# Eight or seven row tiles of a sparse neighbour sum by mask matmuls, the rest by indirect transfers

## The chip, the cores and the metric

One Trainium2 chip, one core of it. A core has five engines that run their own instruction streams: PE (TensorE, matmuls), DVE (VectorE), ACT (ScalarE), POOL (GpSimd) and SP (SyncE), and 16 DMA engines that they feed. The metric is the device time of one execution in microseconds (us), and smaller is better. Times inside an execution are counted from the start of the span, which reaches from the first to the last instruction of the program.

## The reference

Two graph layers over N = 4096 nodes with D = 512 features, float32. The adjacency `adj` is symmetric with the diagonal set and with a chance of about 0.002 for any other pair, so a row has some 9 neighbours on average and 24 at most in the lists below.

```python
h = relu(layernorm(x))
# layer 0: 8 heads; of a row's neighbours the one with the highest score gives its values
attn = softmax(Q K^T * scale + energy, over the neighbours)
x = x + (attn == max(attn)) / 8 @ V
# layer 1: mean over the neighbours, two linear maps, a third over both
h = relu(layernorm(x))
agg = mask @ h / deg
x = x + relu(concat(h @ W_self + b_self, agg @ W_nb + b_nb) @ W_comb + b_comb)
```

The last line is where this document plays: with the weights folded, layer 1 needs `G = h @ wN` for every node and then, for every row, the sum of G over the row's neighbours, times 1/degree, plus the row's own part.

## The kernel before, in words

`sparse_path` does the whole work; `general_path` stands behind a flag for denser inputs and isn't run here. The nodes are sorted by degree, falling. The order is in `perm`, and the sorted rows are cut into 32 tiles of 128 rows. `CAPS[r]` (L509) is the length of the neighbour lists of tile r, with the row itself in slot 0: 24 for tile 0, 11 for tiles 7 to 9, 5 for tile 31.

The kernel has three parts. The first (to about 340 us) reads adj, computes keys and values, packs the adjacency into words and makes the lists. The words are the point here: `W_d` holds for each row 256 words, and bit s of word j (with an offset) says whether node 256 s + j is a neighbour; s runs over NPL = 16 planes. The second part (to about 1075 us) is layer 0 and the products of layer 1, tile by tile; its last steps write G to `G_d` in HBM and the rows' own parts to `X1_d`, fetch the words of the first DENSE tiles (`dense_words`, L1417) and turn them (`dense_turn`, L1424) into `wT`, word by row.

The third part (L1629 to L1740) makes the neighbour sums in two ways at once.

- **By mask**, for tiles 0 to DENSE-1. For each plane s: `dense_mask(s)` (L1638, DVE) shifts one bit of all words to where it reads as the float 2.0 and drops the rest; `dense_keys(s)` (L1648, a DMA on ACT's queue) loads the 256 rows of G of this plane; `dense_sum(s)` (L1655, PE) multiplies, two matmuls per tile and plane, and adds up in one PSUM bank per tile. Masks and keys have three buffers each, so mask s waits until PE has ended plane s-3.
- **By transfers**, for tiles DENSE to 31. For each of the CAPS[r]-1 list places POOL issues one indirect DMA (L1719, in the helper `gather`, L1103) that fetches 128 rows of G. The rows land in `room`, which has three places, taken by r % 3. DVE adds them up (`total`, L1682; for the last tile `halved`, L1691), and `finish` (L1672, L1673) multiplies, adds the own part and the residual. `put` (L1119) scatters the finished tile to the output with another indirect DMA on POOL.

Everything in this part is issued in the order in which the loop at L1713 writes it. After tile r's transfers POOL issues the put of tile r-2; then come tile r's sum and finish on DVE; then, as long as `calls >= pace * (s - 2)`, one more mask and its matmuls, where `calls` counts list transfers plus one for each tile done. Three masks are issued ahead of the loop. So a mask stands on DVE's queue between the finish of one tile and the sum of the next, and a put on POOL's queue holds back all transfers behind it until DVE has finished that tile. In the last pass, POOL's last transfers are followed by the finishes and puts of the first half of the mask tiles, then by tile 31, then by the other half (L1723 to L1739).

Of the kernel before, what the change touches and what calls it, by code (L numbers as in the profile page):

```python
# [512 lines left out]
LISTV = CAPS[VTILE]  # L513
FIRST = 4
GMAX = 10
DENSE = 8
MAGIC = 0x5F3759DF


# [18 lines left out]
def sparse_path(  # L538
# [91 lines left out]
    with ExitStack() as pa:  # L630
# [299 lines left out]
        def on(step, t, *args):  # L930
            if 0 <= t < KT:
                step(t, *args)
# [159 lines left out]
    with ExitStack() as pb:  # L1092
# [9 lines left out]
        def gather(dst, src, idx, at=0):  # L1102
            last[0] = nc.gpsimd.indirect_dma_start(  # L1103
                out=dst, out_offset=None, in_=src,
                in_offset=bass.IndirectOffsetOnAxis(ap=idx, axis=0), element_offset=at,
            )
            if at:

                beyond.append(last[0])
                for w in written:  # L1110
                    tc.declare_no_dep(last[0].ins, w.ins, reason="other columns")
# [305 lines left out]
        def dense_words():  # L1417

            wg = gp.tile([P, DENSE, SEG], F32, tag="kg", name="wg")
            for r in range(DENSE):  # L1420
                gather(wg[:, r, :], W_d[:, :], perm[:, r : r + 1])
            return wg

        def dense_turn(wg):  # L1424

            wT = wp.tile([P, 2, DENSE, P], I32, tag="w_a", name="wT")
            for a in range(0, DENSE, 2):
                pt = pst.tile([P, NC, P], F32, tag="tr", name="tr")
                for h in range(2):
                    for b in range(2):  # L1430
                        nc.tensor.transpose(pt[:, 2 * h + b, :], wg[:, a + b, ts(h, P)], ident)
                nc.vector.tensor_copy(
                    wT[:, :, a : a + 2, :], pt.rearrange("p (h b) q -> p h b q", h=2)
                )
            return wT

# [4 lines left out]
        left, last_tiles, m = apart[FIRST:], fused[-3:], KT - FIRST - 3  # L1441
# [22 lines left out]
        for r in turns:  # L1464
            p = pos[r]
# [28 lines left out]
        def late(step, kind, i, *args):  # L1494

            out_ = []
            for r in turns:
                if plan[kind].get(r) == i:
                    out_ += step(r, *args) or []
            return out_  # L1500
# [22 lines left out]
        for i in range(-5, KT):  # L1523
# [9 lines left out]
            a, b = on(key_gathers, i), late(value_gathers, "value", i)  # L1533
# [86 lines left out]
        fi = cp.tile([1, 1], I32, tag="fi", name="fi")  # L1620
        nc.vector.tensor_copy(fi, fps)
        wT = dense_turn(wg)
        for r in tail:
            s = st[r]
# [4 lines left out]
    with ExitStack() as pd:  # L1629
# [4 lines left out]
        order.enter_context(tc.manual_schedule())  # L1634
        dacc = [psd.tile([P, D], F32, tag=f"da{r}", name="da") for r in range(DENSE)]
        masks, keys = {}, {}

        def dense_mask(s):  # L1638

            mk = gp.tile([P, 2, DENSE, P], F32, tag="mk", name="mk")  # L1640
            nc.vector.tensor_scalar(
# [66 lines left out]
        s = ahead  # L1708
        calls = 0

        pace = 11
        x1s = {}
        for r in range(DENSE, KT):  # L1713
            n = CAPS[r] - 1
# [29 lines left out]
def kernel(tc, *args):  # L1744
    left = sparse_path(tc, *args)
    with tc.If(left > 0):
        general_path(tc, *args)
# [40 lines left out]
```

## Time and profile before

| | us |
|---|---|
| median of 6 runs (lowest to highest) | 1421.24 (1417.43 to 1425.43) |
| the profiled execution's own time | 1419.52 |
| its span | 1417.8 |
| first transfer of the third part, POOL | 1077.46 |
| first and last matmul of the masks, PE | 1114.19 and 1373.1 |
| end of the last list transfer on POOL | 1388.5 |
| mean granted TensorE clock | 0.853 of full speed |

How to read the profile. A page gives, for each engine, its busy time; a picture of the span in 40 slices; the chain of work that ended last; and groups of instructions, one line each: code line, engine, operation, what it writes from what it reads, how many, then busy us and the mean ns of one, then the idle time of the engine ahead of them and what ended it. A view of waits adds up who waited for whom: us in total, times, the longest. A timeline gives single instructions in order: start, duration, engine and line, and in brackets the idle time ahead and its releaser. A table by windows gives, for each stretch of time, each engine's busy time with the number of its instructions, the granted clock, and the share of time in which the DMA engines were busy. A releaser called "issue" means that the engine waited for nothing that the profile shows; "remote" means that the semaphore's change could not be matched to an instruction that ended just then. A float32 matmul leaves two records, so 512 records are 256 matmuls, and a plane of eight tiles is 32 records.

### The profile page before, as it was taken

The page shows a single profiled execution, that of the slowest core. Times are in us where ns is not written, and L with a number is a line of the kernel's source. Part 1 is how long each engine was busy: PE and PEld are TensorE (multiplying, and loading weights), DVE is VectorE, ACT ScalarE, POOL GpSimd, SP SyncE. Part 2 cuts the span into 40 slices and gives each one's busy share as a digit, 9 for nine tenths or more (in the row PEclk, how much of TensorE's full clock was granted, in tenths as well). Part 3 has the DMA queues.
Part 4 walks back from the last instruction along what each step waited for, and adds up shares of the span by engine and source line. Part 5 has one row for each costly group of instructions (what it writes and reads, how often), then busy time and mean ns, then how long its engine had stood idle before and what let it go on. Part 6 is the DMA issues. An engine that isn't in the chain of part 4 may idle for free. (4 is left out here: it accounts for less than half of the span.)

```text
span 1417.8 us, 10765 instructions
## 1 busy us (share of the span) xinstructions
PE 1071.9 (76%) x2918; PEld 487.7 (34%) x2918; DVE 991.3 (70%) x1650; ACT 427.8 (30%) x880; POOL 776.2 (55%) x910
## 2 busy tenths in 40 slices
PE   5998989867763658567788767777889597989870
PEld 3554545423321223222333222333333242434330
DVE  5568786883594498878787787777572494859495
ACT  5787766612200333232333323332531000000000
POOL 2322313244677476666766666667445654775574
PEclk9999999989985778778887778888899797998895
DMA  9999998295765377777777777767555986786763
GB/s 363 419 421 420 419 360 306 99 363 209 221 190 152 95 245 212 227 234 236 229 228 226 218 223 223 224 209 219 208 178 155 354 306 200 237 260 204 233 220 130
DMA packets 109222, 350.09 MB, mean 247 GB/s; under 512 B 18064, under 2 KB 18064, under 8 KB 100960
## 3 DMA queue, kind: packets, MB, share of 16 engines
q0 software_dynamic: 63376, 208.23, 47.3%
q1 hardware_dynamic: 39552, 129.78, 23.7%
q10 hardware_dynamic: 6224, 11.31, 2.4%
q8 instruction: 25, 0.41, 0.1%
q14 instruction: 45, 0.37, 0.1%
HBM read 285.25 MB, written 68.19 MB: 249 GB/s over the span
## 5 line engine op out<-in xcount | busy, mean ns | idle before, releaser
L1660 PE MATMUL da<-gk,mk 128*128 128x512 f32 x512 | 237.8, 622 | 36.8 <-issue 21.3
L628 PE MATMUL q<-wq,hqT 128*128 128x512 f32 x256 | 156.8, 718 | 142.2 <-issue 123.6
L1103 POOL DMA_INDIRECT kg<-K_d,sidx x177 | 170.2, 961 | 76.3 <-issue 54.1
L1103 POOL DMA_INDIRECT room<-G_d,sidx x174 | 176.7, 1015 | 58.0 <-issue 55.7
L1227 DVE TENSOR_REDUCE sc<-pr 128x32 f32<-128x2048 f32 (+3 forms) x114 | 183.3, 1608 | 3.9
L1660 PEld LDWEIGHTS da<-gk,mk 128*128 128x128 f32 x512 | 101.6, 199 | 173.0 <-issue 173.0
L1682 DVE TENSOR_REDUCE acc<-room 128x512 f32<-128x4096 f32 (+5 forms) x23 | 152.5, 6628 | 4.5 <-DMA room<-G_d,sidx 4.4
L1103 POOL DMA_INDIRECT o<-K_d,vi x128 | 123.3, 963 | 39.1 <-issue 38.7
L628 PE MATMUL pg<-swN,hT 128*128 128x512 f32 x216 | 124.1, 728 | 19.6 <-ACT hT L1347 17.4
L628 PEld LDWEIGHTS q<-wq,hqT 128*128 128x128 f32 x256 | 53.3, 218 | 216.3 <-issue 197.1
L628 PE MATMUL pk<-wk,room 128*128 128x512 f32 x256 | 121.1, 617 | 4.4 <-ACT room L810 4.2
L1103 POOL DMA_INDIRECT room<-K_d,sidx x102 | 99.5, 976 | 32.8 <-issue 26.8
L628 PE MATMUL pv<-wv,room 128*128 128x512 f32 x256 | 115.2, 601 | 0.0
L1224 DVE TENSOR_TENSOR pr<-q,kg 128x2048 f32<-128x2048 f32 (+3 forms) x51 | 102.4, 2007 | 1.4
L1360 PE MATMUL pr<-swS,hT 128*128 128x512 f32 x216 | 99.9, 605 | 0.0
L1224 DVE TENSOR_TENSOR pr<-q,room 128x2048 f32<-128x2048 f32 (+3 forms) x42 | 66.8, 1590 | 42.3 <-issue 24.9
L1119 POOL DMA_INDIRECT G_d<-gs,perm x32 | 31.7, 989 | 104.2 <-ACT gs L1366 69.4
L1224 DVE TENSOR_TENSOR pr<-q,km 128x512 f32<-128x512 f32 x21 | 14.4, 687 | 102.5 <-remote 96.6
L1366 ACT COPY gs<-pg 128x512 f32<-128x512 f32 x27 | 15.7, 582 | 226.6 <-remote 214.3
L628 PEld LDWEIGHTS pg<-swN,hT 128*128 128x128 f32 x216 | 49.3, 237 | 99.2 <-issue 65.2
L1260 DVE COPY_PREDICATED o<-best,room 128x512 f32<-128x512 int32 x102 | 74.3, 728 | 5.9 <-DVE o L1260 1.9
L749 ACT ACTIVATE mkt<-adjt,sgb 128x2048 bf16<-128x2048 int32 x37 | 74.2, 2005 | 12.8 <-POOL adjt L670 12.6
(222 smaller groups left out, 1542.6 us busy)
## 6 DMA issues: line engine op xcount, KB each, us to landing
adjt<-adj_dram SPq DMA_DIRECT2D x37, 1024.0 KB
room<-adj_dram SPq DMA_DIRECT2D x27, 1024.0 KB
x<-X_d SPq DMA_DIRECT2D x32, 512.0 KB
xt<-x_dram SPq DMA_DIRECT2D x32, 256.0 KB
K_d<-ks POOLq DMA_DIRECT2D x32, 256.0 KB
X_d<-xo SPq DMA_DIRECT2D x32, 256.0 KB
X_d<-own SPq DMA_DIRECT2D x32, 256.0 KB
gk<-G_d ACTq DMA_DIRECT2D x16, 512.0 KB
```

Of the source, the lines that this page charges most:

```text
L628: nc.tensor.matmul(dst, h[:, c, :], w[:, c, :], start=(c == 0), stop=(c == NC - 1))
L749: nc.scalar.activation(mk, st[t]["adj"][j], AF.Sigmoid, bias=sgb, scale=400.0, accum_out=degs[:, t, j : j + 1],)
L1103: last[0] = nc.gpsimd.indirect_dma_start(out=dst, out_offset=None, in_=src, in_offset=bass.IndirectOffsetOnAxis(ap=idx, axis=0), element_o ...
L1119: new = nc.gpsimd.indirect_dma_start(out=dst, out_offset=bass.IndirectOffsetOnAxis(ap=perm[:, r : r + 1], axis=0), in_=src, in_offset=None,)
L1224: nc.vector.tensor_tensor(pr[:, :g, :], s["q"].unsqueeze(1).to_broadcast([P, g, D]), kk, ALU.mult)
L1227: nc.vector.tensor_reduce(sc[:, g0 : g0 + g, :], pr[:, :g, :].rearrange("p g (h d) -> p g h d", h=H), AX.X, ALU.add,)
L1260: nc.vector.copy_predicated(s["o"].rearrange("p (h d) -> p h d", h=H), best[:, k, :].bitcast(I32).unsqueeze(2).to_broadcast([P, H, HD]), b ...
L1360: nc.tensor.matmul(pr, s["hT1"][:, c, :], wS[:, c, :], start=False, stop=(c == NC - 1))
L1366: nc.scalar.copy(s["gs"], s["pg"])
L1660: nc.tensor.matmul(dacc[r], masks[s][:, h, r, :], keys[s][:, h, :], start=(s == 0 and h == 0), stop=(s == NPL - 1 and h == 1),)
L1682: nc.vector.tensor_reduce(acc, g[:, 0:n, :].rearrange("p n f -> p f n"), AX.X, ALU.add)
```

## The change

DENSE goes from 8 to 7. Tile 7, with 10 list places, joins the tiles that are summed by transfers: the loop starts at 7, and 184 list transfers are issued in place of 174. The masks, their matmuls, the words fetched and turned, the accumulators and the last finishes are of seven tiles. `dense_turn` works in pairs of tiles and so learns to treat a last single one. And `pace` goes from 11 to 13: a new plane of masks is issued for every 13 counted calls. Of the 16 planes, 13 are issued in the loop; before, those were due after tiles 8, 9, 11, 12, 13, 14, 15, 16, 18, 19, 20, 22 and 23, and now they are due after tiles 8, 9, 10, 11, 13, 14, 15, 17, 18, 20, 22, 23 and 25.

```diff
-DENSE = 8
+DENSE = 7
...
             for a in range(0, DENSE, 2):
                 pt = pst.tile([P, NC, P], F32, tag="tr", name="tr")
+                m = min(2, DENSE - a)
                 for h in range(2):
-                    for b in range(2):
+                    for b in range(m):
                         nc.tensor.transpose(pt[:, 2 * h + b, :], wg[:, a + b, ts(h, P)], ident)
                 nc.vector.tensor_copy(
-                    wT[:, :, a : a + 2, :], pt.rearrange("p (h b) q -> p h b q", h=2)
+                    wT[:, :, a : a + m, :],
+                    pt.rearrange("p (h b) q -> p h b q", h=2)[:, :, 0:m, :],
                 )
...
-        pace = 11
+        pace = 13
```

## The prediction

> **What bounds the kernel now.** I read the chain of work that ended last first, because it says which engines carry the end:
>
> ```profile
> issue 3%; POOL 2%; DVE 2%; DMA 1%; POOLq 0%; DVEq 0%
> POOL room L1103 2%; DVE acc L1682 1%; DVE x L1672 1%; DMA room<-G_d,sidx 1%; DMA out_dram<-x,perm 0%; POOL out_dram L1119 0%; DVE x L1673 0%; DVE room L1691 0%; POOLq L1741 0%; DVEq L1682 0%; POOLq L1119 0%; DVEq L1691 0%; DVEq L1672 0%
> ```
>
> It runs along POOL's transfers and DVE's sums; no matmul is on it. Then the page's groups, for the price of one instruction:
>
> ```profile
> L1660 PE MATMUL da<-gk,mk 128*128 128x512 f32 x512 | 237.8, 622 | 36.8 <-issue 21.3
> ...
> L1103 POOL DMA_INDIRECT room<-G_d,sidx x174 | 176.7, 1015 | 58.0 <-issue 55.7 <-DMA room<-G_d,sidx 1.3 <-DMA out_dram<-x,perm 1.0
> ...
> L1682 DVE TENSOR_REDUCE acc<-room 128x512 f32<-128x4096 f32 (+5 forms) x23 | 152.5, 6628 | 4.5 <-DMA room<-G_d,sidx 4.4
> ```
>
> A list transfer costs POOL (176.7 + 58.0) / 174 = 1.35 us with the issue time ahead of it. Then the waits from 1077 us to the end:
>
> ```profile
> DVE mk L1641 <- remote: 56.9, 3, 20.8
> ...
> POOL out_dram L1119 <- DVE x L1673: 54.0, 11, 15.8
> DVE mk L1641 <- PE da L1660: 21.7, 4, 13.5
> ```
>
> The reader should see two waits that belong together: masks on DVE wait for PE, and POOL's puts wait for DVE. DVE's timeline and POOL's, around the longest pair:
>
> ```profile
> 1174.96 0.69 DVE L1673 SCALAR_TENSOR_TENSOR x<-x 128x512 f32<-128x512 f32 x1
> 1196.46 1.23 DVE L1641 TENSOR_SCALAR mk<-wT 128x2048 int32<-128x2048 int32 x1 [20.81 <-remote]
> 1197.60 8.01 DVE L1682 TENSOR_REDUCE acc<-room 128x512 f32<-128x4608 f32 x1
> ```
>
> ```profile
> 1190.67 0.95 POOL L1103 DMA_INDIRECT room<-G_d,sidx  x1 [0.30 <-issue]
> 1207.40 1.72 POOL L1119 DMA_INDIRECT out_dram<-x,perm  x1 [15.78 <-DVE x L1673]
> ```
>
> Mask 6 stands on DVE from 1175.65 to 1196.46; behind it wait tile 13's sum and finish, behind that its put, and behind that POOL's whole queue. POOL stops so four times: 10.53, 15.78, 11.91 and 12.45 us, 50.7 in all. So **POOL carries the third part, and PE, through the masks, decides when POOL stops**. The windows show how PE looks in three of the stops:
>
> ```profile
> 1143.00:1178.00 35.00, 35.00 (x83) 15.51 (x82) 30.83 (x11) 0.00 (x0) 26.81 (x27) 1.00 0.82 272
> 1178.00:1197.00 19.00, 9.45 (x15) 3.22 (x14) 0.54 (x1) 0.00 (x0) 10.53 (x11) 0.67 0.63 203
> ...
> 1264.00:1281.00 17.00, 9.84 (x15) 3.23 (x14) 2.12 (x2) 0.00 (x0) 9.43 (x10) 0.67 0.73 221
> ...
> 1330.00:1342.00 12.00, 7.04 (x11) 2.21 (x10) 0.87 (x1) 0.00 (x0) 5.50 (x6) 0.69 0.61 200
> ```
>
> The first number after the stretch's length is PE's busy time with its records. At full pace a record comes each 0.429 us (35.0 us hold 83); in these stretches 15, 15 and 11 come where 44, 40 and 28 would. Why PE crawls there no row says. But each crawl ends just after POOL has run dry: POOL's last transfers end at 1191.62, 1276.17 and 1337.03, and the waiting masks start at 1196.46, 1278.88 and 1341.13, that is 4.8, 2.7 and 4.1 us later. In the second part it is the same (POOL's last transfer ends at 625.9, ACT's wait for PE at 630.62). I take it that PE is held until POOL's transfers have drained. From POOL's restart to the first plane whose end is told late, by the counted records, are 16 to 29, 35 to 49 and 21 to 35 us. The first stop (10.53) is of another kind: PE started at 1114.19, mask 3 asked for plane 0 at 1117.4 and got it at 1130.88.
>
> **The change part by part.** All against the span of 1417.8 us.
>
> *Transfers.* Ten more, 10 x 1.35 = 13.5 us on POOL, which carries the path; one put more ahead of the last transfer, 1.3 (0.99 and 0.30 of issue). Sum +14.8. Without the stretched ones, 10 x 1.25 + 1.3 = 13.8 is the low end.
>
> *The first stop goes.* Mask 3 was due after the first looped tile, now after the second. By then DVE has done two sums (8.74 and 8.94 us) and two finishes, about 1127.5; plane 0 of 28 records ends near 1114.2 + 6 x 0.855 + 22 x 0.429 = 1128.8. The put that needs tile 8 comes at about 1131. So -10.5; at worst 9 us of it stay, if PE starts later.
>
> *Matmuls and pace.* A plane has 28 records, 12.0 us in place of 13.7; a plane is due per 13 calls, 13 x 1.35 = 17.6 us in place of 14.9. PE, which runs about three planes behind at first, gains: without stalls plane k ends near 1128.8 + 12.0 k, so planes 6, 9 and 12 near 1201, 1237 and 1273. Masks 9, 12 and 15, which ask for them, come after tiles 15, 20 and 25, at 1077.5 + 82, 120 or 153 transfers at 1.35 + 7, 12 or 17 puts at 1.3 + some 4 of landing + sum and finish (8.7, 7.8, 6.9): near 1210, 1267 and 1317. The lead grows from 9 over 30 to 44 us (less where a plane itself waits for its mask). So the short waits (2.1, 2.1 and 3.9 us in before) go, which carried no stop, and a stall shows later on DVE. It still shows, if PE is released only when POOL stops. In before POOL's runs from restart to stop were 49, 69 and 49 us. I take 35 to 48 us to a stall, as in the longest one, and 20 us of running on, as after 1172: with both running from 1114 a first stop near 1175, a restart near 1190, a second stop with the lead of then near 1280, a restart near 1295. POOL then has 1280 - 1077 - 15 = 188 of its 275 us behind it, and some 75 ahead; the last mask is issued 50 ahead of its end, 25 us after the restart, sooner than a third stall. So **two of the three stall stops stay and one goes**: -13.4, their mean. The ends: none goes (0), or all go (-40.1), the latter if a stall has its own length and isn't ended by POOL.
>
> *Masks on DVE.* Each is an eighth shorter (1.23 to about 1.08 us). The trace shows POOL transfers stretched wherever a mask runs beside them (2.33, 1.82, 1.45, 1.59, 1.55 against a median of 0.95), about 8.7 us over all; an eighth is -1.1. [...]
>
> *The tail.* From the last transfer's end to the span's end are 29.3 us, of which the dense finishes go at 1.39 each, one after the other: one fewer, -1.4. Three of seven now stand ahead of tile 31, four behind.
>
> *At nothing:* one fetch of words fewer (1.26 on POOL at the end of the second part) lies ahead of POOL's wait of 10.8 us for ACT; without that cover it would be -1.3. Two transposes and half a copy fewer in `dense_turn` run on PE and DVE while POOL already transfers; uncovered, under 1 us. DVE's extra sum (8.8) and ACT's and SP's queues, unchanged in number, lie beside POOL: per tile of 9 places DVE needs 8.05 + 1.5 and POOL 12.6. A PE that waits for masks late in the part will start them cold. The row: after 15.1 us of idling the first six records came 0.855 us apart, 2.6 us lost. [...] The sum takes nothing for it, as POOL has longer than PE there.
>
> Sum: 1417.8 + 14.8 - 10.5 - 13.4 - 1.1 - 1.4 = 1406.2. The profiled execution's own time is 1.7 over its span, and the median of the runs 1.7 over that: 1409.6, told as 1410.
>
> **Rivals.** (1) *Three stops stay.* For it: restart to stall took 16 to 29 us once, and PE is as busy as before until about 1270. Then 13.4 comes back: 1423, which is no change. (2) *One stall stop or none.* For it: the late lead of 30 to 44 us is longer than the longest mask wait, 20.8. Against it: the crawls ended with POOL's run and not after a fixed time. One stop: 1396; none: 1383. (3) *PE ends last, slower.* The place is the end: the last mask leaves after tile 25, with 31 transfers and 6 puts left, 31 x 1.35 + 6 x 1.3 = 49.7 us. PE may then have three planes, 36 + 2.6 us, 11 us less than POOL. If a crawl begins once no mask waits, nothing stops POOL and PE stays held until the last transfer lands; of 84 records some 20 were still done after a stall began, and 64 x 0.429 = 27.5 us of matmuls remain ahead of the finishes of the mask tiles. That adds up to 28: 1438 with two stops. It decides from a crawl that takes more than those 11 us. Against it: in before PE ended at 1373.1 and 15 us ahead of POOL. (4) *The change doesn't do what it says*: the instruction order shows 224 matmuls for 256, 184 transfers for 174 and 7 word fetches for 8, so no.
>
> **How the numbers follow.** Two stops 0.42 (1410), three 0.25 (1423), one or none 0.16 (1396, 1383), PE last or a fourth stop 0.17 (1438 and about that). A measurement of this kernel tells 0.3% from no change, 4.3 us. Faster (under 1417): one or none, and most of two stops, 0.53. Within: most of three stops and the upper edge of two, 0.20. Slower: the rest of three, and PE last, 0.27. The range reaches from one stop to PE last, 1394 to 1438; the two-stop case alone, with its unknown sizes, spans 1403 to 1418.
>
> **What would show it.** Right: 448 mask records; no POOL stop near 1132; 184 transfers at about 1.35; two waits of puts over 10 us; POOL's last transfer near 1378 and PE's last matmul ahead of it. Wrong: three or four such waits; a wait of a finish for PE after the last transfer (rival 3); "remote" mask waits with no stop of POOL, or stops with no late PE, which would break the coupling I assume.

## The result, and the profile after

The changed kernel takes 1433.75 us (median of 17 runs, 1424.77 to 1463.17), against 1422.29 us for the kernel before in the 38 runs made beside it. The ratio is **1.0077, 95% interval 1.0054 to 1.0101**: 0.8% slower, some 11 us. The forecast was 1410 us and faster. The medians of the runs of before lie between 1422 and 1432 us in the groups below, so all comparisons go by the ratio to the runs of before on the same chip. Some executions of a kernel take a few per cent longer than the rest (up to 1480.54 us for the kernel before), and the ratios leave them out.

The profiled execution of the changed kernel has a span of 1440.4 us, which is long among its runs: 22.6 us over that of before, where the typical difference is 11. The chain of work that ended last, again by engine and by line:

```profile
DVE 3%; issue 2%; another core or an unknown queue 1%; POOL 1%; DMA 1%; POOLq 0%; DVEq 0%
DVE acc L1684 2%; POOL room L1103 1%; DVE x L1674 1%; DMA out_dram<-x,perm 1%; DMA room<-G_d,sidx 0%; DVE x L1675 0%; DVE room L1693 0%; DVE mk L1643 0%; POOLq L1743 0%; DVEq L1684 0%; POOLq L1119 0%; POOL out_dram L1119 0%; DVEq L1674 0%; DVEq L1693 0%
```

Still no matmul in it, but an entry that before did not have: 1% for "an unknown queue". It is one piece of 20.15 us, from 1343.33 to the start of a mask at 1363.51: the wait of that mask for PE. The groups:

```profile
L1662 PE MATMUL da<-gk,mk 128*128 128x512 f32 x448 | 220.9, 644 | 77.9 <-issue 51.0
...
L1103 POOL DMA_INDIRECT room<-G_d,sidx x184 | 183.2, 995 | 57.8 <-issue 54.2
```

The counts are those announced: 448 records, 184 transfers. PE is busy 17 us less, but idles 77.9 us ahead of its records instead of 36.8: it has less to do and is later with it. The waits from 1077 us to the end (in all, times, longest):

```profile
DVE mk L1643 <- remote: 69.9, 3, 26.3
...
POOL out_dram L1119 <- DVE x L1675: 47.0, 11, 15.9
PE da L1662 <- DMA gk<-G_d: 26.9, 1, 26.9
DVE own L1372 <- remote: 22.7, 1, 22.7
...
POOL out_dram L1119 <- DMA x<-X_d: 20.0, 1, 20.0
```

Three long mask waits are still there, each longer (20 to 26 us, before 18 to 21). And the first stop did not go; it is 20.0 us. It has another cause than before, and it lies ahead of all masks. DVE's timeline shows it:

```profile
1097.81 0.75 DVE L1372 SCALAR_TENSOR_TENSOR own<-gs,smeta,pr 128x512 f32<-128x512 f32 x1 [3.99 <-issue]
1121.22 0.75 DVE L1372 SCALAR_TENSOR_TENSOR own<-gs,smeta,pr 128x512 f32<-128x512 f32 x1 [22.67 <-remote]
1124.22 3.10 DVE L1643 TENSOR_SCALAR mk<-wT 128x1792 int32<-128x1792 int32 x3 [2.25 <-DMA X_d<-own]
...
1136.89 0.69 DVE L1675 SCALAR_TENSOR_TENSOR x<-x 128x512 f32<-128x512 f32 x1
```

And POOL's timeline shows the puts that end the first two stops:

```profile
1137.86 1.01 POOL L1119 DMA_INDIRECT out_dram<-x,perm  x1 [19.99 <-DMA x<-X_d]
...
1204.02 1.59 POOL L1119 DMA_INDIRECT out_dram<-x,perm  x1 [14.43 <-DVE x L1675]
```

The "own" products are the rows' own parts, the last work of the second part: PE multiplies, and DVE takes the product up when PE's semaphore tells it that the product is done (the notice). They come every 4.7 us until the last, the fifth, which DVE gets at 1121.22 although PE's last record of it starts at 1101.80. Behind it stand masks 0 to 2, tile 7's sum, its finish (ended at 1137.58) and, on POOL, its put at 1137.86. The profile puts that 19.99 us to the load of x; the timeline says that the put followed the finish at once. POOL's last transfer had ended at 1117.87, 3.3 us before DVE got the product: the same pair as in the three mask stops.

In those too it is the notice that is late, and not the plane. Here are the start of PE's timeline, in which a run of matmuls without a gap is one line, and two of the three waiting masks:

```profile
1129.27 48.61 PE L1662 MATMUL da<-gk,mk 128*128 128x512 f32 x108 [26.87 <-DMA gk<-G_d]
1179.14 0.59 PE L1662 MATMUL da<-gk,mk 128*128 128x512 f32 x1 [1.26 <-issue]
```

```profile
1193.21 1.09 DVE L1643 TENSOR_SCALAR mk<-wT 128x1792 int32<-128x1792 int32 x1 [23.40 <-remote]
...
1290.41 1.09 DVE L1643 TENSOR_SCALAR mk<-wT 128x1792 int32<-128x1792 int32 x1 [26.28 <-remote]
```

They are masks 5 and 10, which wait for planes 2 and 7. A plane is 28 records, so plane 2 is the first 84 records, done near 1167; mask 5 asks for it at 1169.8 and starts at 1193.21. Seven slow records follow the first 108, and then 114 without a gap up to 1245.5, so plane 7 (record 224) was done near 1243, 47 us ahead of mask 10. Plane 11, by the same count, was done near 1329, 34 us ahead of mask 14 at 1363.51. The matmuls themselves slow down only after these planes, from 1178, 1246 and 1340 on. So a spell has two signs, first notices that don't come, then records far apart. "PE is held" below means such a spell.

Broken down for POOL, from its first list transfer to its last (gaps of its timeline over 2.6 us count as stops):

| | before | after |
|---|---|---|
| first list transfer starts, us | 1077.46 | 1080.35 |
| first stop | 10.5 | 20.0 |
| other stops | 15.8, 11.9, 12.4 | 14.4, 15.9, 13.0 |
| the rest (transfers, puts, small gaps) | 260.4 | 267.9 |
| from the last transfer's end to the end | 29.3 | 28.8 |

So 12.7 of the 22.6 us of this profile are longer stops (9.5 of them the first), 7.5 are the transfers and the put, 2.9 the later start, and 0.5 came back in the tail.

### The profile page after: what moved, and what is told of

It is laid out like the page before. It is cut to its first block, busy times and chain, and to the rows that moved or that the text cites. A ratio compares the mean times of both kernels' runs of the same rounds, so it can differ in the third digit from the quotient of the medians.

```text
span 1440.4 us, 10657 instructions
## 1 busy us (share of the span) xinstructions
PE 1043.2 (72%) x2852; PEld 474.1 (33%) x2852; DVE 997.2 (69%) x1651; ACT 427.7 (30%) x880; POOL 782.1 (54%) x918
## 5 line engine op out<-in xcount | busy, mean ns | idle before, releaser
L1662 PE MATMUL da<-gk,mk 128*128 128x512 f32 x448 | 220.9, 644 | 77.9 <-issue 51.0
L628 PE MATMUL q<-wq,hqT 128*128 128x512 f32 x256 | 147.9, 691 | 123.7 <-issue 101.7
L1103 POOL DMA_INDIRECT room<-G_d,sidx x184 | 183.2, 995 | 57.8 <-issue 54.2
L1684 DVE TENSOR_REDUCE acc<-room 128x512 f32<-128x4096 f32 (+5 forms) x24 | 161.2, 6717 | 8.1 <-DMA out_dram<-x,perm 3.1
L1662 PEld LDWEIGHTS da<-gk,mk 128*128 128x128 f32 x448 | 91.3, 204 | 207.5 <-issue 207.2
L1103 POOL DMA_INDIRECT room<-K_d,sidx x102 | 100.1, 981 | 33.6 <-issue 26.5
L749 ACT ACTIVATE mkt<-adjt,sgb 128x2048 bf16<-128x2048 int32 x37 | 74.2, 2007 | 12.6 <-POOL adjt L670 12.4
L1224 DVE TENSOR_TENSOR pr<-q,km 128x512 f32<-128x512 f32 x21 | 14.4, 685 | 88.9 <-remote 47.0
```

Of the source, the lines that this page charges most:

```text
L628: nc.tensor.matmul(dst, h[:, c, :], w[:, c, :], start=(c == 0), stop=(c == NC - 1))
L749: nc.scalar.activation(mk, st[t]["adj"][j], AF.Sigmoid, bias=sgb, scale=400.0, accum_out=degs[:, t, j : j + 1],)
L1103: last[0] = nc.gpsimd.indirect_dma_start(out=dst, out_offset=None, in_=src, in_offset=bass.IndirectOffsetOnAxis(ap=idx, axis=0), element_o ...
L1224: nc.vector.tensor_tensor(pr[:, :g, :], s["q"].unsqueeze(1).to_broadcast([P, g, D]), kk, ALU.mult)
L1662: nc.tensor.matmul(dacc[r], masks[s][:, h, r, :], keys[s][:, h, :], start=(s == 0 and h == 0), stop=(s == NPL - 1 and h == 1),)
L1684: nc.vector.tensor_reduce(acc, g[:, 0:n, :].rearrange("p n f -> p f n"), AX.X, ALU.add)
```

## The experiments

Kernels e1 to e3 and e5 were run together on one chip, then e4 and e6 to e8 on another, then e9 to e12, then e13 and e14.

### Which half of the change costs: e1 and e2

```
e1 = before, with          e2 = after, with
-        pace = 11         -        pace = 13
+        pace = 13         +        pace = 11
```

> Eight mask tiles, a plane per thirteen transfers (only the pace of the change). Theory T (the loss is the ten transfers and one put, 14.8 us on POOL; POOL's stops add up to the same as in the kernel before, some 50 us, whatever the pace): no change against the kernel before, 1418 to 1427 us, and again four stops of POOL over 10 us. Rival P (the slower pace makes the stops longer, as in the profile of the changed kernel, where they add up to 63 us against 50.7): 1428 to 1438 us. What the prediction held (pace 13 takes the first stop and one more away): 1395 to 1408 us.

Measured: 1413.24 us, ratio 0.9958 (0.991 to 1.0006). Rival P falls. The pace alone does not cost; by the value it **gains 6 us**, though the interval just reaches no change. Theory T's four stops are not there either. The waits:

```profile
DVE mk L1641 <- remote: 47.2, 3, 22.4
POOL out_dram L1119 <- DVE x L1673: 35.4, 11, 15.2
```

Two stops are left, 15.2 and 13.8 us. POOL's first run goes on past 1132 with a pause of 1.9 us only. So with eight tiles the pace did to the stops what the prediction said of it: the first goes, and one of the three others.

> Seven mask tiles, a plane per eleven transfers (only the tile of the change). Theory T: the loss is all here, 1430 to 1438 us, with four stops of POOL over 10 us. Rival P: 1418 to 1428 us, since PE has an eighth less to do per plane at the old pace and the transfers are paid back by shorter stops.

Measured: 1431.8 us, ratio 1.0132 (1.009 to 1.0175). Theory T holds by the time: the loss is all in the seven tiles, some 19 us. But its sum is too small (14.8 less 2.5), and the stops are not those of before: three over 10 us in place of four (18.5, 16.5 and 14.5, and one of 4.8), and for the first of them DVE waits 20.3 us for the last own product, as in the changed kernel. By the values, the pace (0.42% less) and the tile (1.32% more) nearly add up to the whole change (0.77% more).

### Is PE held until POOL stops: e3, e5 and e4

```
e3:  mk = gp.tile(..., tag="mk", name="mk")   ->   ..., name="mk", bufs=6)
```

> The changed kernel with six buffers for mask planes instead of three: mask s waits for plane s-6 in place of s-3. Theory H (PE is held while POOL's transfers run and is let go only when they stop): PE gets slow 35 to 40 us after POOL's restart and stays slow until a mask wait stops POOL, one or two planes later than now; stops get fewer (two), PE ends later: 1415 to 1440 us. Theory L (a slow spell of PE has its own length of 15 to 50 us, whatever POOL does): three planes of slack, 3 x 17.6 = 53 us, cover all of them: no stop of POOL over 5 us but the first, 1385 to 1400 us.

Measured: 1435.24 us, ratio 1.0152 (1.0112 to 1.0191). Theory L falls: three planes more of slack make it slower.

```profile
POOL out_dram L1119 <- DVE x L1675: 63.6, 11, 17.9
...
DVE mk L1643 <- PE da L1662: 30.4, 1, 30.4
...
DVE mk L1643 <- remote: 22.3, 1, 22.3
```

POOL's run after the first stop lasts 111 us in place of 52, and PE is slow for the last 67 of them; then it stops 17.5 us, and 13.9 later. Two stops, as theory H has it, and what is saved in stops is lost at the end: PE's last record starts at 1431.7, 23 us after POOL's last list transfer.

```
e5:  mask s >= 3 is written to a tile of its own that nobody reads;
-    dacc[r], masks[s][:, h, r, :], keys[s][:, h, :]
+    dacc[r], masks[s % 3][:, h, r, :], keys[s][:, h, :]
```

> The changed kernel, but PE multiplies masks 0, 1 and 2 over and over, and DVE writes the later masks, at the same places and cost, into tiles that nobody reads; so DVE and POOL never wait for PE before the end. Leaves out: the right masks of planes 3 to 15. Theory H (PE is let go only by a stop of POOL): POOL runs through to about 1375, PE is slow (a record in 2.1 us) from some 40 us after its start to POOL's end, and has some 260 of 448 records, 110 us, left then: 1470 to 1510 us. Theory L (slow spells of their own length): PE needs 193 us and some spells of 20 us each, ends near POOL: 1380 to 1405 us, no stop of POOL but the first.

Measured: 1503.52 us, ratio 1.0644 (1.0595 to 1.0693); **theory H, inside its range**. PE in four stretches (length, PE busy with its records, PEld, DVE, ACT, POOL, then the granted clock, the DMA share and GB/s):

```profile
1130.00:1160.00 30.00, 30.00 (x71) 13.30 (x70) 29.79 (x13) 0.00 (x0) 23.03 (x23) 1.00 0.91 329
1200.00:1230.00 30.00, 10.11 (x10) 3.14 (x11) 21.54 (x9) 0.00 (x0) 22.99 (x24) 0.50 0.74 231
1300.00:1330.00 30.00, 10.11 (x10) 3.16 (x11) 22.28 (x12) 0.00 (x0) 23.30 (x23) 0.50 0.68 212
1400.00:1430.00 30.00, 30.00 (x71) 13.26 (x70) 0.00 (x0) 0.00 (x0) 0.00 (x0) 1.00 0.17 52
```

PE starts at full pace, drops to a record in 3 us some 45 us after POOL's restart, and stays there for 200 us, with nothing that it waits for, until POOL is done (1360.4). Records follow each other without a gap again from 1372. POOL ran 233 us without a stop, and the finishes of the mask tiles then waited 114 us for PE.

A rival is near at hand: the granted clock is halved in these stretches. But at the half clock records came 0.855 us apart in the kernel before (six in the 5.13 us from 1114.19, granted clock 0.50), which would be 35 in 30 us and not 10. And in the changed kernel the first gap, ahead of 1179.14, falls where the clock is still full (1.00 from 1176 to 1180, 0.64 in the next 4 us). So do the first gaps of its two later spells, ahead of 1246.22 and 1340.36 (1.00 from 1243 to 1247 and from 1336 to 1340, 0.80 and 0.70 in the next 4 us). In all three the half clock follows the gaps.

e4 asks the reverse, how long POOL takes when PE has nearly nothing to do:

```
e4 (in dense_sum):
+    if r and (s or h):
+        continue
```

> The changed kernel with PE summing only the first of the seven mask tiles (of the others only the first product): 38 products in place of 224. Leaves out: most of six mask tiles' sums. If the late notices of PE are all that stops POOL after its start, the three stops of 12 to 16 us go, 43 us in the changed kernel's profile: 1380 to 1395 us, and no stop of POOL over 5 us but the first. If another wait takes their place (DVE's sums, landings), 1410 us or more.

Measured: 1405.68 us, ratio 0.9861 (0.9803 to 0.992). POOL's only long wait is the first stop (18.0 us), the three others are gone and nothing took their place, as the first theory said. Its number was too low because I took the 43 us of the long profiled execution from the median; from the profile's own 1442 it is 1399, and this profile's span is 1398.4.

### What of POOL's work holds PE: e6, e7, e14

```
e6 = e5 with
-    gather(gg[:, i, :], G_d[:, :], sidx[:, r, i + 1 : i + 2])
+    nc.sync.dma_start(gg[:, i, :], G_d[ts((r + i) % KT, P), :])
e7 = e5 with
+    gather(gg[:, i, 0:16], G_d[:, :].rearrange("n (a f) -> (n a) f", f=16), ...)
e14 = e5 with
-    acc = (total if r < KT - 1 else halved)(gg, n)
+    acc = gg[:, n - 1, :]
```

> Like e5 (nobody waits for PE before the end), with the list transfers of the third part issued by SP as plain loads of 128 rows of 2 KB, the same bytes, in place of POOL's indirect ones; POOL issues only puts. Leaves out: the right rows and the right masks. Theory D (POOL's own work on indirect transfers holds PE): PE runs its 448 records 0.43 us apart, some 195 us from about 1120, and the time is below 1390 us. Theory B (the traffic itself holds PE): PE is slow while the loads run, as in e5, and ends well after them: over 1420 us.

> Like e5, but each list transfer fetches 64 bytes per row in place of 2 KB: as many indirect transfers and packets, 1/32 of the bytes. Leaves out: most of each row, and the right masks. Theory D: PE is held as in e5, a record in about 2 us until POOL stops, 1470 to 1510 us. Theory B: PE runs at 0.43 us a record, and the time is that of POOL, 1370 to 1400 us.

> Like e5 (nobody waits for PE before the end), and DVE's sums of the list tiles are left out as well: a list tile is finished from its last neighbour alone. Leaves out: the list sums and the right masks. DVE then has only masks and finishes, some 2 us per tile. If POOL's transfers alone hold PE: a record in 2 to 3 us from some 40 us after POOL's start to its end, 1460 to 1510 us. If it takes DVE's sums beside them: PE at 0.43 us a record all through, 1360 to 1390 us.

Measured, one run each: e6 1385.56, e7 1520.11, e14 1511.95 us. A stretch of each, in that order, in the middle of the transfers:

```profile
1180.00:1210.00 30.00, 30.00 (x71) 13.30 (x70) 29.79 (x12) 0.00 (x0) 4.19 (x5) 1.00 1.04 394
```

```profile
1300.00:1330.00 30.00, 11.04 (x12) 3.16 (x11) 25.52 (x12) 0.00 (x0) 23.07 (x23) 0.50 0.14 32
```

```profile
1200.00:1230.00 30.00, 11.13 (x11) 3.17 (x11) 4.02 (x6) 0.00 (x0) 22.75 (x24) 0.50 0.81 261
```

In e6 the same bytes come by SP's plain loads, the DMA engines are full (share 1.04, 394 GB/s), and PE runs at full pace (71 records in 30 us) with full clock (1.00); its last record starts near 1325. In e7 POOL issues as many indirect transfers for 1/32 of the bytes, the DMA share is 0.14, and PE is held as in e5 (12 records in 30 us). In e14 DVE does next to nothing (4.02 of 30 us), and PE is held as well (11 records). So **POOL's indirect transfers hold PE**, not the traffic and not DVE beside them. (e6 is no version of the kernel: plain loads can't follow the lists.) Whether it is POOL's issuing or the indirect form that matters, these runs don't separate, as in e6 both are gone. The times of e7 and e14 lie 10 and 2 us above the ranges expected, in the direction of more holding.

### Why the first stop grew: e10 and e13

The loop over list tiles starts at tile `DENSE`, and the place of a tile's transfers in `room` is `r % 3`. With eight mask tiles the first tile takes the third place, with seven the second. The third place overlaps the rows from which PE's last own products still read, so there POOL has to pause for PE. In the kernel before, that pause and the last own product are:

```profile
1090.00 0.95 POOL L1103 DMA_INDIRECT room<-G_d,sidx  x1 [1.49 <-issue]
```

```profile
1099.18 0.75 DVE L1372 SCALAR_TENSOR_TENSOR own<-gs,smeta,pr 128x512 f32<-128x512 f32 x1 [3.93 <-issue]
```

```
e10 = after with           e13 = before with
-    r % 3                 -    r % 3
+    (r + 1) % 3           +    (r + 2) % 3
```

> The changed kernel with the rooms of the transfers in the order 2, 0, 1 as in the kernel before (where tile 8 comes first), in place of 1, 2, 0: the seventh to tenth transfers then write where PE's last own products still read, and POOL pauses some 1.5 us for PE at the tenth, as in the kernel before. Theory G (that pause is what lets PE's notice of the last own product come in time): the first stop of 17 to 20 us goes, 1410 to 1420 us. Rival N (it has nothing to do with the rooms): 1428 to 1438 us, first stop as now.

> The kernel before (eight tiles, pace 11) with the rooms in the order 1, 2, 0 for its tiles 8, 9, 10, as the changed kernel has them for 7, 8, 9. Theory G (the rooms decide whether POOL pauses for PE at the tenth transfer, and so whether the last own product is told in time): DVE's wait for the last own product becomes some 20 us, the keys come 10 us later, the first stop grows from 10.5 to 17 to 20 us, and the time by 0.4 to 1.0%. Rival N: the own products are told in time as before, and the time stays within 0.3%.

In e10 POOL pauses at the tenth transfer, as in before, and DVE gets the last own product in time:

```profile
1091.23 0.95 POOL L1103 DMA_INDIRECT room<-G_d,sidx  x1 [1.41 <-issue]
```

```profile
1100.41 0.75 DVE L1372 SCALAR_TENSOR_TENSOR own<-gs,smeta,pr 128x512 f32<-128x512 f32 x1 [3.94 <-issue]
```

In e13, the kernel before with that one edit, it is late as in the changed kernel, and no such pause is in POOL's timeline:

```profile
1118.63 0.75 DVE L1372 SCALAR_TENSOR_TENSOR own<-gs,smeta,pr 128x512 f32<-128x512 f32 x1 [21.01 <-remote]
```

The rooms decide when the last own product is told, both ways. That the pause is the means is inferred from its being there in one pair and absent in the other. The times: e13 1434.26 us, ratio 1.0040 (1.0002 to 1.0079), as theory G expected; its first stop is 21.7 us. e10 1429.16 us, ratio 0.9983 (0.9933 to 1.0032), 0.9% under the changed kernel, with intervals that do not overlap. But by its time alone e10 would fall to rival N (1428 to 1438), and theory G's 1410 to 1420 was a miss: the stop at 1118 is gone, POOL's first run is then 68 us long, PE is held in it, and an 11.8 us stop comes at 1146.9, ahead of 16.5 and 13.9.

### Can POOL let PE go more cheaply: e8, e12, e11, e9

```
e8 = after with, behind the transfers of tile r:
+    if r % 3 == 0:
+        seen = dp.tile([P, GMAX], F32, tag="seen", name="seen", bufs=1)
+        nc.gpsimd.tensor_copy(seen[:, 0:n], gg[:, 0:n, 0])
e12 = e8 with a memset of 128x2048 in place of the copy
e11 = e8 with the rooms of e10      e9 = e1 with the copy where r % 3 == 1
```

> The changed kernel with a small copy on POOL after the transfers of tiles 9, 12, 15 and so on to 30 (eight of them), which reads one column of the tile's rooms, so that POOL waits until all its transfers have landed, about 3 us each, 24 us in all. If a short stop of POOL lets PE go and the 35 to 40 us start anew, no mask is late and the three stops (43 us) go: 1408 to 1418 us. If PE needs a longer stop, nothing goes and 24 us come: 1450 to 1460 us.

Measured: 1418.14 us, ratio 0.9960 (0.9916 to 1.0004), 1.2% under the changed kernel. The drains cost 27.6 us; PE is still held for the last 3 to 12 us before two of them, but after the first stop no mask stops POOL for longer than a drain does.

> The changed kernel with a memset of 128x2048 on POOL (1.8 us) at the eight places of e8, in place of the copy that waits for landings: POOL does not issue for some 2 us but waits for nothing. If a short pause in POOL's issuing is enough to let PE go, the three stops go (43 us) and 17 come: 1402 to 1412 us. If POOL's transfers must have landed, or the pause must be longer: the stops stay and 17 us come, 1445 to 1455 us.

Measured: 1436.01 us, ratio 1.0041 (1.0005 to 1.0076). Neither: one of the three stall stops goes (15.0 and 12.5 us are left, and a first stop in two pieces of 6.6 and 12.6), which just about pays for the pauses. A pause of 1.8 us without waiting for the landings lets PE go only in part; whether it is too short or lacks the landings stays open.

> e10 with the drains of e8. Under theory G both gains add: 1432 less 17 for the first stop less 14 for the drains, 1398 to 1406 us. Under rival N: as e8, 1414 to 1422 us.

Measured: 1418.74 us, ratio 0.9940 (0.9903 to 0.9978): a miss, no better than e8. The first drain waits 10.6 us for a load of x, about where the first stop was.

> Eight mask tiles, a plane per thirteen transfers (as in e1) and a drain of POOL, as in e8, after the transfers of tiles 10, 13 and so on to 28 (seven, some 25 us). e1 has two stops of 14 to 15 us, 29 us. If drains let PE go, they go, and 25 come: 1405 to 1415 us, little better than e1 at 1413. If e8 gained by something else than fewer holds of PE: above 1430 us.

Measured: **1405.18 us, ratio 0.9836 (0.9777 to 0.9895)**, the best of all and ahead of both kernels. Its waits:

```profile
POOL seen L1723 <- DMA room<-G_d,sidx: 19.2, 6, 3.5
DVE mk L1641 <- remote: 16.8, 2, 15.4
...
POOL seen L1723 <- DMA x<-X_d: 11.2, 1, 11.2
...
POOL out_dram L1119 <- DVE x L1673: 1.9, 5, 0.6
```

POOL's puts wait 1.9 us for DVE, against 54.0 before: what stops POOL is the drains alone. There are eight, as tile 31 has one too, and they take 33.6 us in place of the 25 expected; the first alone is 11.2 us, as long as the first stop was. That e9 beats e1 rests on the ratios of two chips, whose intervals (up to 0.9895, and from 0.991) only just part; the profiled execution of e1 has the shorter span, 1401 against 1405 us.

## Why the prediction was wrong, by its steps

- **What bounds the kernel**: right, and now shown. POOL carries the third part (e4: with hardly any of PE's work it is 20 us faster than before, and no more), and PE is held by POOL's transfers and let go when they stop (e5, e6, e7, e14). What I took from three pairs of times is the mechanism.
- **Transfers, +14.8**: too large for the profile. Everything but the stops grew by 7.5 us, and the 184 transfers cost (183.2 + 57.8) / 184 = 1.31 us each, not 1.35. Masks (-1.1) and tail (-1.4, measured -0.5) were small.
- **The first stop goes, -10.5: this step failed.** "At worst 9 us of it stay" was no bound: it grew to 20.0. The reasoning about mask 3 was right (e1: with eight tiles the stop goes). What it left out is ahead of the masks: DENSE also sets where the loop starts, and with it the room of the first transfers. POOL, which before paused for PE's last own products at its tenth transfer, ran on; PE's last notice came 19 us late, and masks, keys and the first tile's sum with it. No line of the diff shows this edit; e13 shows it alone, e10 undone.
- **One of three stall stops goes, -13.4: this step failed too**; three stayed, 43.4 us against 40.1. It failed on its own, since e10, where the last own product is told in time, still has three (11.8, 16.5, 13.9). Two of its terms were off. A subtraction was wrong: 275 less 188 is 87 us of POOL's work ahead after the second stall stop, not 75, so the last mask would leave some 37 us after the restart and not 25, within the 35 to 48 that I took to a stall. And those 35 to 48 were too long: counted as in the prediction, from POOL's restart to the planes whose end was last told in time and first told late, the changed kernel has 17 to 29, 27 to 39 and 17 to 29. In the changed kernel's profile POOL had 111 us to go after the second stall stop (98 without the third), and mask 14 met a third spell 43 us into them. With eight tiles the pace does take one stall stop away (e1 has two).
- **Rivals**: rival 1 (three stops stay, 1423) had the number of stall stops right, but with the first stop gone. The chances name a fourth stop beside rival 3 (0.17 together), and four is the count that came; but nothing had the first stop grow. Rival 3 (PE ends last) did not come in the changed kernel, where PE's last record starts 11 us ahead of POOL's last list transfer's end; its mechanism is e3's and e5's. Rival 4 was right to be excluded: the counts came out as planned.
- **The sum**: the median lies in the range (1394 to 1438), but the direction was wrong, and the 1410 was 24 us off. In the profile the stops were to shrink by 23.9 and grew by 12.7, 36.6 us of error; all other terms together came out 2.4 us below their forecast.
- **PE's cold starts at nothing**: right for the path, as PE's last record started 11 us ahead of the end of POOL's last list transfer. The row behind them has 15.1 us of idling ahead of the half clock. In e7's held stretch, where PE is busy 11 of 30 us, the granted clock is 0.50 for all 30 us although no wait of PE there is longer than 3.2 us.

## What to carry to other kernels

Where an engine's late notices come in spells, look for what else runs in exactly those spells and ends with them; then a wait that stops that neighbour is not only a cost but the release, and taking it away only moves the debt: more buffers moved it to the end in e3, and in e5, where nobody waits, it came to 114 us there. A short drain on purpose, placed before the spell would stop anyone, was worth more here than three more planes of slack (e8 against e3). And when a constant is changed, follow every expression that holds it: here a loop's start moved buffers by one place, and that cost 0.4% (e13 against before) to 0.9% (the changed kernel against e10), no small part of the whole.

## What the runs showed of the hardware

- PE beside POOL's indirect transfers: in the mask spells of the kernels before and after, 38 to 61 us after POOL's restart, PE falls from a record in 0.43 us to one in 1.7 to 2.5 us on average, and in e5, after some 45 us, to one in 3 us, where it stays until POOL stops, 200 us later. Its notices stop coming earlier, in the changed kernel 17 to 39 us after the restart. Beside SP's plain loads of the same bytes PE kept its full pace (e6: 71 records in 30 us at a DMA share of 1.04). No run here shows where PE is held.
- In the held spells PE's records started at multiples of about 0.70 us after each other (3.50 and 2.11 here in e5's timeline; 3.50, 1.43, 2.81 and 2.09 from 1181.27 on in the changed kernel):

```profile
1349.79 1.01 PE L1663 MATMUL da<-gk,mk 128*128 128x512 f32 x1 [1.09 <-issue]
1353.29 1.01 PE L1663 MATMUL da<-gk,mk 128*128 128x512 f32 x1 [2.49 <-issue]
1355.40 1.01 PE L1663 MATMUL da<-gk,mk 128*128 128x512 f32 x1 [1.10 <-issue]
```

- The release: in the changed kernel's three mask stops the waiting mask started 4 to 6 us after POOL's last transfer, after runs of 52 to 80 us. In e5, after a run of 233 us, PE's records came without a gap again 12 us after POOL was done.
- **What stays open**: what PE shares with POOL's transfers; what sets the time until its notices stay out (the last own product, done 22 us after POOL's first list transfer, lies in the same 17 to 39 us as the planes); and, if POOL's pause is the means in e10, how 1.4 us of it put that off. Every execution here was recorded in the same way, so none tells whether the recording has a part in it.
